# A macaron block (FFN, neighbourhood attention, FFN): new places for the value products, projections, sums and second FFN in the slot plan

## The chip, the cores and the metric

The kernel runs on one core of one Trainium2 chip. The metric is the device time of one execution in microseconds (us), lower is better. Before the change the median of three runs is 2293.7 us (2293.59 to 2294.9).

## The reference

The input is x, 4 batches of 4096 rows of 512 numbers. Three steps follow each other, each with a residual:

```python
x = x + 0.5 * ffn(layernorm(x))        # quantised to blocks of 32, one 512x512 matrix and a bias
x = x + attention(layernorm(x))        # 16 heads of 32; each row sees 13 neighbouring rows
x = x + 0.5 * ffn(layernorm(x))        # the same matrix and bias again
```

In `ffn` both operands are scaled in blocks of 32 to a 6-bit grid of values, multiplied back and then multiplied with each other. In `attention` q, k and v are 512x512 projections; the score of a row with each of its 13 neighbours gets a relative bias, softmax runs over the 13, the probabilities weight the neighbours' v, and a last 512x512 projection follows.

## The kernel before

**Tiling.** The 16384 rows are 128 tiles of 128 rows. Four tiles make a group of 512 rows; a group has four attention items, one for each set of four heads, so there are also 128 items. An item covers 16, 17 or 18 query blocks of 30 rows with windows of 42 keys.

**Exact products out of 16-bit halves.** Operands are split into a high and a low 16-bit part. `product` (line 137) makes one 128x512 result of 12 matmuls (three pairings of parts, four slices of 128). A tile or item needs six such results: `pmf1` (first FFN), `pmv` (values), two `pmqk` (queries and keys of an item), `pmo` (output projection) and `pmf2` (second FFN). Besides there are the scores `ps` (L458, 64 to 72 small matmuls) and the weighted values `pv` (L549, as many). With 18 blocks `pv` is too small and a second result `pw` is taken from the same three buffers as the six products (`ps_m`, three PSUM buffers); `ps` and `pv` have places of their own.

**The slot plan.** The order of all work is written out. Time is cut into slots, seven to a step (`STEP = 7`), and in each step one tile and one item advance by one stage. A stage is a Python generator. `begin(slot, stage, rank)` enters it; within a slot stages run by rank, and `yield n, rank` puts the rest of a stage n slots later. Each engine gets its instructions in the order in which the slots issue them and works through its queue in that order; semaphores make it wait for data and for buffers. Line 607 sets the slots of a tile or item: first FFN `F1`, values `V`, query and key projection `QK`, scores `SC`, weighted values `PV`, output projection `OUT`, and the second FFN `F2` slots behind `OUT`. `out_slot` and `second_slot` place the last tiles by themselves.

**Who does what.** TensorE (PE) does the products. ScalarE (ACT) takes the high parts out of PSUM (L379, L307, L576), normalises (L226, L284), does the exponential (L511) and the copies of the probabilities (L522, L523). GpSimd (POOL) does the adds of biases to x (L610), the two scalings of the quantiser (L239, L244), the small norm factors (L179 to L188) and three passes over the scores (L509, L518, L525). VectorE (DVE) does the rest: low parts (L383, L308, L582, L197), residual adds out of PSUM (L272, L595), statistics (L173, L174), the block maxima and their reciprocals (L232 to L237), the score sums (L500, L503), maxima (L507) and the sums of the probabilities (L514 to L516). SyncE (SP) issues loads, stores and transposing transfers.

**The order in the middle of the kernel**, for one step, as the built program has it:

- PE: ps, pmo, pmqk0, pv, pmqk1, pmf1, pmv, pmf2
- DVE: L507, L173, L174, L595, L173, L174, L197 hlq, L197 hln, L383 qf, L582, L514, L515, L516, L383 qk, L232, L233, L237, L272 (pmf1), L173, L174, L308, L272 (pmf2), L500, L503
- POOL: L179, L182, L185 (second norm), L610, L244, L525, L509, L179, L182, L187, L188 (quantised norms), L610 after_b, L610, L518, L239

A buffer of `ps_m` is free when DVE has taken the low part or the sum out of it. In items of 16 or 17 blocks `pmf1` goes into the buffer that `pmo` held, `pmv` into that of `pmqk0`, `pmf2` into that of `pmqk1`, `pmo` into that of `pmf1`.

Of the kernel before, what the change touches and what calls it, by code (L numbers as in the profile page):

```python
# [63 lines left out]
def macaron_kernel(  # L64
# [67 lines left out]
    def bc(t, n):  # L132

        return t.unsqueeze(2).to_broadcast([t.shape[0], t.shape[1], n])
# [4 lines left out]
    def product(pm, lhs, rhs):  # L139

        n = 0
        for a, b in ((0, 1), (1, 0), (0, 0)):
            for c in range(KC):
                nc.tensor.matmul(  # L144
                    pm, lhs(a, c), rhs(b, c), start=(n == 0), stop=(n == 3 * KC - 1)
                )
                n += 1
# [7 lines left out]
    def begin(slot, stage, rank=5):  # L155
        slots.setdefault(slot, []).append((rank, stage))
# [159 lines left out]
    def span(j):  # L316

        q0 = min(j * QN, length - QN)
        return q0, min(max(q0 - NS, 0), length - KN)

    def kind(j):
        return 1 if j == 0 else 2 if j == n_blocks - 1 else 0

    def late(j):

        return QR - QN if j == n_blocks - 1 else 0
# [11 lines left out]
    def straight(n):  # L338

        return -(-n // 2)  # L340
# [5 lines left out]
    n_items = n_batch * NG * KC  # L346
    qk, probs, stacks = {}, {}, {}

    def item_of(m):

        g, c = divmod(m, KC)
        return g // NG, g % NG, c
# [88 lines left out]
    def softmax(m):  # L441

        b, g, c = item_of(m)
        j0, j1 = group_blocks[g]
        n = j1 - j0
        tq, tk = qk.pop(m)
        ps = ps_s.tile([P, 2, 2, 2, 256], F32, tag="s", name=f"ps{m}")
        half = straight(n)
        for a in range(half):
            for part, sides in ((0, 2), (1, 1)):  # L450
                for i in range(a, n, half):
                    q0, k0 = (KN + at - g * GT for at in span(j0 + i))
                    q0 -= late(j0 + i)
                    u, w = divmod(a, PSB)
                    for r in (0, 2 * D):
                        rows = slice(r, r + 2 * D)
                        o = r if i < half else 2 * D - r
                        nc.tensor.matmul(  # L458
                            ps[o : o + 2 * D, i // half, u, :sides, w * KN : (w + 1) * KN],
                            tq[rows, part, 2 * q0 : 2 * (q0 + QR)],  # L460
                            tk[rows, :sides, k0 : k0 + KN],
                            start=part == 0, stop=part == 1,
                        )

        yield 1, 9
        sf = sfp.tile([P, MAXB, KN], F32, tag="sf", name=f"sf{m}")

        both = sf[:, : 2 * half, :].rearrange("p (v w) k -> p v w k", v=2)

        def parts(special):  # L470

            for w, e in ((0, PSB), (PSB, half)):
                lone = [(v, x) for v, x in special if w <= x < e]
                for v, x in lone:
                    yield slice(v, v + 1), slice(x, x + 1), 2 + v
                two = min(e, n - half)
                w0 = w + (1 if (0, w) in lone else 0)
                two -= 1 if (1, two - 1) in lone else 0
                if w0 < two:
                    yield slice(0, 2), slice(w0, two), 0  # L480
                for v, x, y in ((0, two, e), (1, w, w0)):
                    y = min(y, (half, n - half)[v])
                    if x < y and not (v == 0 and (v, x) in lone):
                        yield slice(v, v + 1), slice(x, y), v

        def sums(v, w, side):

            u, x = divmod(w.start, PSB)
            t = ps[:, v, u, side, x * KN : (x + w.stop - w.start) * KN]
            return t.rearrange("p v (w k) -> p v w k", k=KN)  # L490

        special = []
        if kind(j0) == 1:
            special.append((0, 0))
        if kind(j1 - 1) == 2:
            special.append((1, n - half - 1))
        for v, w, k in parts(special):
            o = both[:, v, w, :]
            bias = table[:, k : k + v.stop - v.start, c, :].unsqueeze(2).to_broadcast(o.shape)
            nc.vector.tensor_tensor(o, sums(v, w, 0), bias, ALU.add)  # L500
        for v, w, _ in parts([]):
            o = both[:, v, w, :]
            nc.vector.tensor_tensor(o, o, sums(v, w, 1), ALU.add)  # L503
        yield 1, 2
        s = sf[:, :n, :]
        top = sm.tile([P, MAXB], F32, tag="top", name=f"top{m}")
        nc.vector.tensor_reduce(top[:, :n], s, AX.X, ALU.max)  # L507
        yield 1, 4
        nc.gpsimd.tensor_tensor(s, s, bc(top[:, :n], KN), ALU.subtract)  # L509
        yield 1, 9  # L510
        nc.scalar.activation(s, s, AF.Exp, scale=alpha)  # L511
        yield 1, 4
        total = sm.tile([P, MAXB], F32, tag="total", name=f"total{m}")
        nc.vector.tensor_reduce(total[:, :n], s, AX.X, ALU.add)  # L514
        nc.vector.reciprocal(total[:, :n], total[:, :n])  # L515
        nc.vector.tensor_tensor(total[:, :n], total[:, :n], p_scale[:, :n], ALU.mult)  # L516
        yield 1, 4
        nc.gpsimd.tensor_tensor(s, s, bc(total[:, :n], KN), ALU.mult)  # L518
        yield 2, 8
        p = p_tile  # L520
        ph = p[:, :n, :KN]
        nc.scalar.copy(ph, s)  # L522
        nc.scalar.copy(p[:, :n, 2 * KN : KV], ph)  # L523
        yield 2, 4
        nc.gpsimd.tensor_tensor(p[:, :n, KN : 2 * KN], s, ph, ALU.subtract)  # L525
        pT = ptp.tile([P, MAXB, P], F16, tag="pT", name=f"pT{m}")
        nc.sync.dma_start_transpose(out=pT[:, :n, :], in_=p[:, :n, :].rearrange("p n k -> p (n k)"))
        probs[m] = pT
# [58 lines left out]
    def project_out(t, slot):  # L587

        r = t * P % RING
        pm = ps_m.tile([P, dim], F32, tag="mm", name=f"pmo_{t}")  # L590
        product(
            pm, lambda s, c: ring[:, s, c, r : r + P], lambda s, c: wt[:, s, c, PO : PO + dim]
        )
        yield 1, 8
        nc.vector.scalar_tensor_tensor(xs[t], pm, cp, xs[t], ALU.mult, ALU.add)  # L595
        moments(slot, t, "n3")

    def second_half(t):

        yield from ffn(t, "f2")  # L600
        nc.sync.dma_start(out=of[t * P : (t + 1) * P, :], in_=xs.pop(t))


    EARLY = 3
    STEP = 7

    F1, V, QK, SC, PV, OUT, F2 = 5, 2 * STEP + 6, 5 * STEP + 3, 6 * STEP, 8 * STEP + 3, 13 * STEP + 2, 12

    def add_bias(t, b):
        nc.gpsimd.tensor_tensor(xs[t], xs[t], b, ALU.add)  # L610
# [8 lines left out]
    HELD = range(NT - 15, NT - 7)  # L619
    LAST = NT - GROUP - 1  # L620

    def out_slot(t):


        i = t - LAST
        if i >= 0:
            return (n_items - 1) * STEP + PV + 3 + 2 * i
        if i >= 1 - GROUP:
            return LAST * STEP + PV + 21 + 4 * i
        return t * STEP + OUT  # L630

    def second_slot(t):

        i = t - LAST
        if t in HELD:
            return (n_items - 1) * STEP + PV - (16, 13, 10, 6, 5, 4, 3, 2)[t - HELD[0]]
        if i in (-2, -1):
            return out_slot(NT - 1) + 3 + i
        return out_slot(t) + F2

    for t in range(NT):
        k = t * STEP
        sooner = (0, 2, 5, STEP)[t] if t <= EARLY else 0
        begin(k - 18 - (STEP if t == EARLY else 0), one(load, t), 0)
        slot = k - 10 - (10 if t == EARLY else 0)
        enlist(slot, t, "n1")
        if not 0 < t < EARLY:
            begin(slot - 1, one(moments, slot, t, "n1"), 1)
        begin(k + F1 - sooner, first_half(t))
        begin(k + V, values(t))  # L650
        begin(k + F1 - sooner, one(add_bias, t, half_ffn_b), 8)
        at = out_slot(t)
        begin(at - 5, one(add_bias, t, after_b), 8)
        enlist(at + 2, t, "n3")
        begin(at, project_out(t, at + 2))
        begin(at + 6 if t < LAST else second_slot(t) - 2, one(add_bias, t, half_ffn_b), 8)
        begin(second_slot(t), second_half(t))
    for slot in together:
        if together[slot][0][0][1] == "n3" or together[slot][0][0][0] >= EARLY:
            begin(slot, quantised_norms(slot), 1)  # L660
    for m in range(n_items):
        k = m * STEP
        begin(k + QK, project_qk(m))
        begin(k + SC, softmax(m), 6)
        begin(k + PV, attend(m), 6)
    for n in range(n_batch * NG):
        k = n * GROUP * STEP
        b, g = divmod(n, NG)
# [4 lines left out]
    with tc.tile_pool(name="setup", bufs=1) as sp, tc.tile_pool(name="scratch", bufs=2) as scr:  # L673
# [23 lines left out]
        for o in chunks:  # L697
            w, i = (qkv_w, o) if o < 3 * KC else (proj_w, o - 3 * KC)
# [145 lines left out]
        for turned in (0, 2):  # L844
            for h in range(4):
                at = row_of(h ^ turned)
# [41 lines left out]
        slot = first  # L888
# [49 lines left out]
```

## Time and profile before

| what | us |
|---|---|
| median of three runs | 2293.7 |
| the profiled execution | 2295.28 |
| its span, which the profile shows | 2293.5 |
| PE busy in the span | 2214.2 (97%) |
| DVE busy | 2011.7 (88%) |
| POOL busy | 1969.2 (86%) |
| ACT busy | 1695.5 (74%) |
| chain of work that ended last: PE's share | 87% |

The mean granted clock of PE in the profiled execution is 0.993 of full speed. In the lists that follow a line gives the start in us from the beginning of the span, the busy time, the engine, the source line and the operation with output and inputs; `xN` counts merged instructions, and a bracket tells idle time just before and who ended it.

### The profile page before, as it was taken

The page shows a single profiled execution, that of the slowest core. Times are in us where ns is not written, and L with a number is a line of the kernel's source. Part 1 is how long each engine was busy: PE and PEld are TensorE (multiplying, and loading weights), DVE is VectorE, ACT ScalarE, POOL GpSimd, SP SyncE. Part 2 cuts the span into 40 slices and gives each one's busy share as a digit, 9 for nine tenths or more (in the row PEclk, how much of TensorE's full clock was granted, in tenths as well). Part 3 has the DMA queues.
Part 4 walks back from the last instruction along what each step waited for, and adds up shares of the span by engine and source line. Part 5 has one row for each costly group of instructions (what it writes and reads, how often), then busy time and mean ns, then how long its engine had stood idle before and what let it go on. Part 6 is the DMA issues. An engine that isn't in the chain of part 4 may idle for free.

```text
span 2293.5 us, 65425 instructions
## 1 busy us (share of the span) xinstructions
PE 2214.2 (97%) x26771; PEld 1052.9 (46%) x26771; DVE 2011.7 (88%) x3769; ACT 1695.5 (74%) x2544; POOL 1969.2 (86%) x2006
## 2 busy tenths in 40 slices
PE   3799999999999999999999999999999999999978
PEld 1344444444444444444444444444444444444433
DVE  6899998888988988898988998888988988989775
ACT  5697777777777777777777777777777777777752
POOL 4588988988988988888888888888888889888776
PEclk9999999999999999999999999999999999999989
DMA  7687776777767777777776776777776777866654
GB/s 201 153 178 161 162 160 154 159 162 158 160 156 155 164 162 154 161 158 157 162 158 155 162 161 154 160 157 155 164 160 151 167 158 154 166 155 147 137 107 104
DMA packets 926213, 359.61 MB, mean 157 GB/s; under 512 B 719452, under 2 KB 890328, under 8 KB 925912
## 3 DMA queue, kind: packets, MB, share of 16 engines
q1 hardware_dynamic: 925568, 354.90, 70.8%
q8 instruction: 209, 3.42, 0.6%
q14 instruction: 92, 0.75, 0.1%
q10 hardware_dynamic: 344, 0.53, 0.1%
HBM read 110.26 MB, written 67.29 MB: 77 GB/s over the span
## 4 chain that ended last, share of the span: by engine, by line
PE 87%; DVE 7%; ACT 2%; POOL 2%; DMA 1%; issue 1%; SPq 0%; ACTq 0%; DVEq 0%; POOLq 0%
PE pmqk L144 27%; PE pmf L144 26%; PE pmo L144 14%; PE pmv L144 13%; PE ps L458 4%; PE pv L549 3%; DVE stn L173 1%; DVE hlq L197 1%; DVE hln L197 1%; DVE sc L232 1%; ACT qk L390 0%; DVE x L272 0%; POOL yq L239 0%; DVE total L514 0%; DVE qf L383 0%
## 5 line engine op out<-in xcount | busy, mean ns | idle before, releaser
L144 PE MATMUL pmf<-wt,xT 128*128 128x512 f16 x3048 | 702.7, 381 | 13.3 <-DMA xT<-hlq 7.4
L144 PE MATMUL pmqk<-x,wt 128*128 128x512 f16 x3072 | 705.8, 379 | 0.4 <-DVE after_b L836 0.4
L144 PEld LDWEIGHTS <-xT 128*128 128x128 f16 x3048 | 298.4, 98 | 377.2 <-DMA xT<-hlq 15.2
L144 PEld LDWEIGHTS <-wt 128*128 128x128 f16 x3072 | 289.7, 98 | 336.0 <-issue 1.3
L239 POOL TENSOR_TENSOR yq<-yq,r 128x1024 f32<-128x1024 f32 (+1 forms) x141 | 247.1, 1752 | 135.6 <-DVE r L237 124.1
L144 PE MATMUL pmv<-wt,x 128*128 128x512 f16 x1536 | 353.9, 380 | 4.2 <-DVE qf L383 2.6
L144 PE MATMUL pmo<-wt,ring 128*128 128x512 f16 x1536 | 357.2, 383 | 0.0
L390 ACT ACTIVATE qk<-qf,parity 128x1024 f16<-128x1024 f16 x256 | 349.3, 1432 | 0.0
L610 POOL TENSOR_TENSOR x<-x,half_ffn_b 128x512 f32<-128x512 f32 x256 | 327.8, 1281 | 0.0
L272 DVE SCALAR_TENSOR_TENSOR x<-pmf,coef,x 128x512 f32<-128x512 f32 x256 | 180.0, 703 | 144.7 <-PE pmf L144 141.1
L576 ACT ACTIVATE ring<-pv 128x510 f16<-128x510 f32 (+7 forms) x176 | 78.7, 475 | 307.3 <-PE pv L549 234.4
L173 DVE BATCH_NORM_STATS2 stn<-x 128x6 f32<-128x512 f32 x384 | 265.2, 691 | 8.8 <-DMA x<-in_L_attn_x_dram 0.2
L244 POOL TENSOR_TENSOR yq<-q,sc 128x1024 f32<-128x1024 fp8e4 (+1 forms) x141 | 246.2, 1746 | 4.8 <-ACT q L242 4.8
L144 PEld LDWEIGHTS <-x 128*128 128x128 f16 x1536 | 150.5, 98 | 186.9 <-issue 4.9
L242 ACT ACTIVATE q<-yq,nudge 128x1024 fp8e4<-128x1024 f32 (+1 forms) x141 | 150.0, 1064 | 115.9 <-POOL yq L239 107.6
L144 PEld LDWEIGHTS <-ring 128*128 128x128 f16 x1536 | 141.2, 98 | 160.5 <-issue 5.0
L518 POOL TENSOR_TENSOR sf<-sf,total 128x714 f32<-128x714 f32 (+2 forms) x128 | 178.7, 1396 | 37.2 <-DVE total L516 19.3
L226 ACT ACTIVATE yq<-x,nbq,rsq 128x512 f32<-128x512 f32 x254 | 193.1, 803 | 16.7 <-POOL nbq L185 15.2
L525 POOL TENSOR_TENSOR p<-sf,p 128x714 f16<-128x714 f32 (+2 forms) x128 | 192.5, 1504 | 0.0
L509 POOL TENSOR_TENSOR sf<-sf,top 128x714 f32<-128x714 f32 (+2 forms) x128 | 182.4, 1425 | 3.5 <-DVE top L507 3.3
L197 DVE TENSOR_TENSOR hlq<-yq,hlq 128x1024 f16<-128x1024 f32 (+1 forms) x141 | 167.6, 1189 | 8.7 <-ACT hlq L193 6.6
L610 POOL TENSOR_TENSOR x<-x,after_b 128x512 f32<-128x512 f32 x128 | 162.9, 1274 | 0.0
(143 smaller groups left out, 3441.0 us busy)
## 6 DMA issues: line engine op xcount, KB each, us to landing
vs<-vd SPq DMA_DIRECT2D x144, 357.0 KB
x<-in_L_attn_x_dram SPq DMA_DIRECT2D x128, 256.0 KB
vd<-vt SPq DMA_DIRECT2D x128, 256.0 KB
out_dram<-x SPq DMA_DIRECT2D x128, 256.0 KB
vs<-vd SPq DMA_DIRECT2D x24, 378.0 KB
vs<-vd SPq DMA_DIRECT2D x24, 315.0 KB
rows<-in_L_attn_qkv_w_dram SPq DMA_DIRECT2D x12, 256.0 KB
xT<-hlq SPq DMA_TRANSPOSE x141
```

The source lines that it names most:

```text
L144: nc.tensor.matmul(pm, lhs(a, c), rhs(b, c), start=(n == 0), stop=(n == 3 * KC - 1))
L173: nc.vector.bn_stats(st, xs[t])
L197: nc.vector.tensor_tensor(hl[:, :, 1, :], y, hl[:, :, 0, :], ALU.subtract)
L226: nc.scalar.activation(y[:, u], xs[t], AF.Identity, bias=nb[:, u : u + 1], scale=rs[:, u : u + 1])
L239: nc.gpsimd.tensor_tensor(yb, yb, bc(r, QB), ALU.mult)
L244: nc.gpsimd.tensor_tensor(yb, q8.rearrange("p u (n q) -> p (u n) q", q=QB), bc(sc, QB), ALU.mult)
L272: nc.vector.scalar_tensor_tensor(xs[t], pm, cf, xs[t], ALU.mult, ALU.add)
L390: nc.scalar.activation(to, whole[0], AF.Copy, scale=parity[:, e : e + 1])
L509: nc.gpsimd.tensor_tensor(s, s, bc(top[:, :n], KN), ALU.subtract)
L518: nc.gpsimd.tensor_tensor(s, s, bc(total[:, :n], KN), ALU.mult)
L525: nc.gpsimd.tensor_tensor(p[:, :n, KN : 2 * KN], s, ph, ALU.subtract)
L610: nc.gpsimd.tensor_tensor(xs[t], xs[t], b, ALU.add)
```

## The change

Every stage keeps its instructions; their places in the plan change.

- `attend` (pv) starts at `9 * STEP` in place of `8 * STEP + 3`, with rank 7: right behind the scores of the item three later. For the last three items it starts four slots sooner than that.
- `project_out` starts two slots later (`OUT`), with rank 7, behind `second_half`, which comes four slots later (`OUT` and `F2` by two each), with rank 6. Both now stand behind the second `pmqk`.
- In `softmax` the sums of the probabilities come one slot later, the copies three (one of them from the sums, two more), the low part four.
- The quantised norm of a new tile comes two slots later (from tile 4 on).
- The last tiles keep their places: `LAST_PV` holds the old value of `PV`, `82` and `12` replace expressions that would have moved.

The orders in the middle of the kernel, as the built program has them:

- PE: ps, pv, pmqk0, pmqk1, pmf2, pmo, pmf1, pmv
- DVE: L507, L197 hln, L383 qf, L173, L174, L272 (pmf2), L595, L173, L174, L383 qk, L197 hlq, L514, L515, L516, L272 (pmf1), L173, L174, L308, L232, L233, L237, L500, L503, L582
- POOL: L179, L182, L185 (second norm), L239, L509, add of half_ffn_b, L244, add of half_ffn_b, L179, L182, L187, L188 (quantised norms), add of after_b, L525, L518

`pmo` now goes into the buffer that `pmqk0` of the same step held, `pmf1` into that of `pmf2`, `pmv` into that of `pmo`; in items with 18 blocks `pmf2` goes into the buffer of `pw`, elsewhere into that of `pmv`.

```diff
@@ softmax
         nc.scalar.activation(s, s, AF.Exp, scale=alpha)
-        yield 1, 4
+        yield 2, 4
         total = sm.tile([P, MAXB], F32, tag="total", name=f"total{m}")
...
         nc.gpsimd.tensor_tensor(s, s, bc(total[:, :n], KN), ALU.mult)
-        yield 2, 8
+        yield 4, 8
         p = p_tile
...
-        yield 2, 4
+        yield 3, 4
         nc.gpsimd.tensor_tensor(p[:, :n, KN : 2 * KN], s, ph, ALU.subtract)
@@ the plan
-    F1, V, QK, SC, PV, OUT, F2 = 5, 2 * STEP + 6, 5 * STEP + 3, 6 * STEP, 8 * STEP + 3, 13 * STEP + 2, 12
+    F1, V, QK, SC, PV, OUT, F2 = 5, 2 * STEP + 6, 5 * STEP + 3, 6 * STEP, 9 * STEP, 13 * STEP + 4, 14
+
+    LAST_PV = (n_items - 1) * STEP + 8 * STEP + 3
@@ out_slot
-            return (n_items - 1) * STEP + PV + 3 + 2 * i
+            return LAST_PV + 3 + 2 * i
-            return LAST * STEP + PV + 21 + 4 * i
+            return LAST * STEP + 82 + 4 * i
@@ second_slot
-            return (n_items - 1) * STEP + PV - (16, 13, 10, 6, 5, 4, 3, 2)[t - HELD[0]]
+            return LAST_PV - (16, 13, 10, 6, 5, 4, 3, 2)[t - HELD[0]]
-        return out_slot(t) + F2
+        return out_slot(t) + (F2 if t < LAST else 12)
@@ entering the stages
-        slot = k - 10 - (10 if t == EARLY else 0)
+        slot = k - (8 if t > EARLY else 20 if t == EARLY else 10)
-        begin(at, project_out(t, at + 2))
+        begin(at, project_out(t, at + 2), 7)
-        begin(second_slot(t), second_half(t))
+        begin(second_slot(t), second_half(t), 6)
-        begin(k + PV, attend(m), 6)
+        begin(k + (PV if m < n_items - 3 else PV - 4), attend(m), 7)
```

## The prediction

> **What bounds the kernel now.** I read the busy times first, then the stretches of 100 us, then one step of the middle in order of time. Busy share and stretches (sums of PE, weight loads, DVE, ACT, POOL; clock; DMA):
>
> ```profile
> PE 2214.2 (97%) x26771; PEld 1052.9 (46%) x26771; DVE 2011.7 (88%) x3769; ACT 1695.5 (74%) x2544; POOL 1969.2 (86%) x2006
> ```
>
> ```profile
> 1000.00:1100.00 100.00, 100.00 (x1242) 47.85 (x1240) 89.57 (x166) 76.58 (x114) 89.22 (x88) 1.00 0.72 157
> ...
> 2200.00:2300.00 100.00, 78.71 (x744) 35.44 (x744) 61.17 (x111) 34.08 (x52) 65.91 (x73) 0.92 0.42 96
> ```
>
> In the middle PE never rests, so a step lasts as long as PE's own work: pmo starts at 1001.53, the next at 1018.65, 17.11 us apart, at full clock. DVE and POOL have about a tenth left; only the end is loose. One step, in order of time:
>
> ```profile
> 1001.53 2.76 PE L144 MATMUL pmo<-wt,ring 128*128 128x512 f16 x12
> ...
> 1004.14 2.75 PE L144 MATMUL pmqk<-x,wt 128*128 128x512 f16 x12
> ...
> 1006.82 0.69 PE L549 MATMUL pv<-pT,vs 126*32 126x30 f16 x68
> 1006.86 1.20 DVE L197 TENSOR_TENSOR hlq<-yq,hlq 128x1024 f16<-128x1024 f32 x1
> 1007.03 1.08 POOL L179 TENSOR_SCALAR rsq<-mv 128x2 f32<-128x2 f32 x1 [0.16 <-DVE mv L174]
> ...
> 1007.45 2.76 PE L144 MATMUL pmqk<-x,wt 128*128 128x512 f16 x12
> ...
> 1007.98 0.68 DVE L197 TENSOR_TENSOR hln<-yn,hln 128x512 f16<-128x512 f32 x1
> ...
> 1008.20 1.04 POOL L182 TENSOR_TENSOR rsq<-rsq,minus_half 128x2 f32<-128x2 f32 x1
> ...
> 1008.92 0.75 DVE L383 SCALAR_TENSOR_TENSOR qf<-pmqk,qk_b,qf 128x512 f16<-128x512 f32 x1 [0.26 <-ACT qf L379]
> ...
> 1009.78 1.27 POOL L610 TENSOR_TENSOR x<-x,after_b 128x512 f32<-128x512 f32 x1
> ...
> 1010.04 2.75 PE L144 MATMUL pmf<-wt,xT 128*128 128x512 f16 x12
> ...
> 1010.19 0.89 DVE L514 TENSOR_REDUCE total<-sf 128x17 f32<-128x714 f32 x1
> ...
> 1011.01 1.27 POOL L610 TENSOR_TENSOR x<-x,half_ffn_b 128x512 f32<-128x512 f32 x1
> 1011.11 0.27 DVE L515 RECIPROCAL total<-total 128x17 f32<-128x17 f32 x1
> ...
> 1011.41 0.91 DVE L516 TENSOR_TENSOR total<-total,p_scale 128x17 f32<-128x17 f32 x1
> ```
>
> Two things matter. A product followed by a product takes 2.59 (1007.45 to 1010.04); followed by pv it takes 2.68 (1004.14 to 1006.82). And L516, 17 numbers a partition, is busy 0.91, up to 0.04 after POOL's add ends (1012.28). In the drained end, with POOL idle, and over all 128:
>
> ```profile
> 2183.07 0.18 DVE L516 TENSOR_TENSOR total<-total,p_scale 128x18 f32<-128x18 f32 x1
> ```
>
> ```profile
> L516 DVE TENSOR_TENSOR total<-total,p_scale x128: 175/894/1279, 105.6 to 2230.8; 128x17 f32<-128x17 f32 x80, 128x18 f32<-128x18 f32 x32, 128x16 f32<-128x16 f32 x16
> ```
>
> (minimum/median/maximum in ns). So L516 waits for the POOL instruction under way, up to 1.10 us. The reverse shows too: L179 takes 1.08 under L197, but 0.19 at 1016.86 without it.
>
> **The change, part by part.**
>
> *PE's own work.* Nothing is added; pv moves from between two products to behind ps. One change from product to small matmuls goes: 0.09 an item. The change back (pv's 0.63 and ps's 0.73 hold about 0.12 of it, the gap from the last ps at 1001.42 to pmo) is replaced by ps to pv, which no row shows. Bounds: all of the 0.12 stays, or it goes too (pv to pw, in one layout, starts after 0.008). The gain is thus 0.09 to 0.20; I take 0.10, since ps and pv use the array in different shapes (64\*64, 126\*32) as product and pv do. PE alone would make 17.01 a step.
>
> The Trainium skill, "TensorEngine Tiling (Array Packing)", section Key Properties, speaks against more: a change of tiling mode, not merely of tile, drains the array, and ps to pv is such a change. By that rule three of the four changes an item stay and the sum is the low end; without it, the high end.
>
> *The new queue of DVE, and a ring through PE.* This decides. After the change pmo goes into the buffer of its own step's pmqk0, so it waits for L383 qf. In DVE's new order, L595, which empties pmo, stands ahead of everything up to the next L383 qf. So pmo, L595, the rest of DVE's queue, L383 qf, pmo is a closed ring. Before, the reader of qf's buffer was pmv, at 1012.63, 2.96 after L383 qf ended (1009.67), and slack covered it. The ring's length from start-to-start times in this step: L595 0.76, L173 0.73, L174 0.10, L383 qk 0.66, L197 hlq 1.12, L514 0.92, L515 0.30, L516 0.10 without a wait (as at 2183.07), L272 0.68, L173 0.73, L174 0.10, L308 0.59 (0.67 less the 0.08 by which neighbours overlap), L232 1.24, L233 0.23, L237 0.27, L500 0.95, L503 0.94, L582 0.60, L507 0.82, L197 hln 0.60, L383 qf 0.75: 13.19. With pmo's 2.76 and two semaphores (0.05, 0.04) the ring is 16.04. It stays hidden below PE's 17.01 only while its waits for POOL sum to under 0.97.
>
> *Waits in the ring.* L516: 0 to 1.10 by the row above. In the new order POOL's L182, L187, L188 and the add of after_b follow the end of an L197 as they do here: from 1008.66 to the add at 1009.78 is 1.12. L516 follows L197 hlq by 0.92 + 0.30 less 0.08 = 1.14. The add starts 0.02 ahead, so L516 meets nearly all of it: I take 1.10. L233 reads two SBUF inputs as L516 does; here it runs at 0.19 (1014.14) beside an idle POOL, afterwards beside L179 and L182 of the second norm (0.19 and 0.57): 0 to 0.57, I take 0.28. L197 hln now stands right behind L507, whose end also releases POOL's L509: DVE is first, so POOL loses some 0.4, which its tenth covers. L197 hlq: 0 (as here), at most L182's 0.57. Ring: 16.04 + 1.10 + 0.28 = 17.42, 0.31 above 17.11.
>
> The Trainium skill, "SBUF — State Buffer", section "SBUF: two separate sides", says the port pair of DVE and POOL is an exclusive lock held for a whole instruction, whoever starts first. That would give L516 no wait at all if it came 0.02 sooner: ring 16.32 by that turn, hidden; 17.42 by the row.
>
> *Items with 18 blocks* (32 of 128). There pmf2 must wait for L582 of pw, before pmo: L507, L197, L383 (2.17) leave the ring, a product (2.59) enters, +0.42, for about 24 items in the middle.
>
> *SP and the softmax moves.* The sums, copies and low part move 1, 3 and 4 slots, pv four: the transposing transfer of p has the time to pv that it had, and loads of value stacks find their buffer free in the slot plan. DMA share 0.72: I cost it at nothing; if a stack were late, about 3 us each in 64 (the longest wait of pv for vs was 3.0).
>
> *Ramp and end.* Steps of the first eight items last 11 to 13 us and DVE queues there too: 0 to 1.3 more each (the two waits), I take 5 in all. In the end pmf2 and pmo now stand where PE waited 4.09 for ACT's L390 (two such gaps), but the last pv come together later: -8 to +12, I take +4.
>
> *Sum.* Middle items, 16 to 124: 108 x 0.31 = 33; 18 blocks 24 x 0.42 = 10; ramp 5, end 4: +52 on the span of 2293.5. The profiled execution (2295.28) lies 1.8 above its span and 1.6 above the median 2293.7, so the difference goes onto the median: 2346, rounded to 2344 as the near tie will not go the bad way every time.
>
> **The rivals.** *PE stays the bound* (the gain arrives). For it: PE is at 100% and a hidden ring costs nothing; the tie at L516 is 0.02 wide. Against: with PE as bound DVE drifts against POOL, and L516 or L197 meets another add. Time: 2293.7 - 117 x 0.10 (0.09 to 0.20: 10.5 to 23) + 9 for ramp and end = 2291, from 2279 to 2299 (with up to 16 there). It holds if ring waits stay under 0.97.
>
> *Half of it:* L516 waits its old median, 0.89 - 0.18 = 0.71, L233 0.28: ring 17.03, so only items with 18 blocks (24 x 0.4) and ramp and end pay, less 108 x 0.08: about 2304. For it: that is what L516 does now. Against: the order around it is new.
>
> *It does not do what it says:* no; the built order has pv behind ps in every item.
>
> *Worse:* POOL, 89% busy, with L509 and L182 held by L197, closes a ring too; L516 1.10, L233 0.57, L197 0.57 give 18.28, +126. For it: POOL's slack is only a tenth; against: all three at once in every step.
>
> **How the numbers follow.** No change that a measurement of this kernel can tell is within 0.2%, 2289.1 to 2298.3. Long ring 0.62 (own range 2316 to 2364; 2316 is L516 1.10 and L233 without a wait: ring 17.14, +3, and 19 for blocks, ramp and end), half 0.20, PE bound 0.13, worse 0.05. Of the PE-bound case 0.07 is faster, 0.05 same, the rest slower; half gives 0.02 same. Together faster 0.07, same 0.07, slower 0.86. The range runs from 2293, within the PE-bound case, to 2364, where L233 waits its whole 0.57 (108 x 0.29 = 31 above the sum, of which I keep 18).
>
> **What would show it.** Right: the middle's steps 17.3 to 17.6 apart, PE below 100% with its idle time before pmo released by DVE L383 qf, L516's median above 1.1, L233 above 0.19, pv 0.1 sooner behind ps than behind a product. Wrong: PE at 100% with steps near 17.0, or idle time before another line (a transfer, L390, POOL).

## The result, and the profile after

The changed kernel takes 2310.8 us (median of four runs, 2310.5 to 2315.1) against 2294.3 of the kernel before on the same chip (2293.6 to 2295.0): ratio 1.0079, interval 1.0066 to 1.0091. It is slower, by 16.5 us, where 50 were forecast. The profiled run took 2310.68 and its span is 2308.7, 15.2 above the span of before.

The busy times of the changed kernel, first part of the page:

```profile
PE 2208.2 (96%) x26771; PEld 1064.1 (46%) x26771; DVE 1950.2 (84%) x3769; ACT 1688.9 (73%) x2544; POOL 1932.6 (84%) x2006
```

PE has the same instructions and is busy 6.0 us less while the span is 15.2 longer, so its idle time grew by 21. Where the loss lies is told by the starts of `ps` in the two timelines (us between the starts of the items named):

| stretch | before | after | difference |
|---|---|---|---|
| start to item 0 | 97.2 | 97.9 | +0.7 |
| items 0 to 8 | 97.1 | 107.2 | +10.2 |
| items 8 to 16 | 138.8 | 141.1 | +2.3 |
| items 16 to 124 | 1839.3 | 1837.9 | -1.4 |
| item 124 to the end | 121.1 | 124.6 | +3.5 |

The middle, where the forecast had its loss, is even a little shorter; the ramp lost. The waits of PE over the whole span (total, times, longest, in us):

```profile
PE ps L458 <- ACT qk L390: 21.6, 13, 3.6
...
PE pv L549 <- DMA pT<-p: 5.9, 1, 5.9
PE pv L549 <- issue: 5.8, 4, 2.9
...
PE pmo L144 <- DVE qf L383: 0.6, 2, 0.5
```

The wait that was forecast, of `pmo` for L383 qf, is the last line: 0.6 us in all. Three others are the story: `ps` for L390 (12.7 before), the last `pv` but one for its transposed probabilities, and "issue", idle time that no semaphore explains.

One step of the middle in order of time (start, busy time, in us):

```profile
1004.08 0.75 DVE L383 SCALAR_TENSOR_TENSOR qf<-pmqk,qk_b,qf 128x512 f16<-128x512 f32 x1
...
1005.41 2.75 PE L144 MATMUL pmo<-wt,ring 128*128 128x512 f16 x12
...
1008.20 0.75 DVE L595 SCALAR_TENSOR_TENSOR x<-pmo,coef,x 128x512 f32<-128x512 f32 x1 [1.84 <-PE pmo L144]
...
1010.26 0.71 POOL L182 TENSOR_TENSOR rsq<-rsq,minus_half 128x2 f32<-128x2 f32 x1
...
1010.45 1.22 DVE L197 TENSOR_TENSOR hlq<-yq,hlq 128x1024 f16<-128x1024 f32 x1
...
1012.00 1.27 POOL L612 TENSOR_TENSOR x<-x,after_b 128x512 f32<-128x512 f32 x1
...
1012.81 0.50 DVE L516 TENSOR_TENSOR total<-total,p_scale 128x17 f32<-128x17 f32 x1
```

`pmo` starts 0.58 after L383 qf ends (1004.83): the ring has slack, and DVE idles 1.84 ahead of L595. The add of after_b starts 0.81 ahead of L516, not 0.02 as forecast, so L516 meets only its tail and takes 0.50.

The ramp, item 5 (order of time):

```profile
154.40 0.89 DVE L507 TENSOR_REDUCE top<-sf 128x17 f32<-128x714 f32 x1
...
155.36 1.76 POOL L509 TENSOR_TENSOR sf<-sf,top 128x714 f32<-128x714 f32 x1 [2.07 <-DVE top L507]
...
157.16 0.89 ACT L511 ACTIVATE sf<-sf,coef 128x714 f32<-128x714 f32 x1 [0.71 <-POOL sf L509]
...
157.96 0.67 ACT L379 ACTIVATE qk<-pmqk,qk_b 128x512 f16<-128x512 f32 x1
...
159.03 2.73 ACT L390 ACTIVATE qk<-qf,parity 128x1024 f16<-128x1024 f16 x2
...
161.81 0.78 PE L458 MATMUL ps<-qk 64*64 64x84 f16 x66 [1.63 <-ACT qk L390]
```

This is a second ring: from `ps` of one item (148.05) over L500 (152.01), L503, L507, POOL's L509 and ACT's queue (L511 stands ahead of L379, and that ahead of L390) to the next `ps`, whose first two matmuls ran at 159.96 and which goes on at 161.81, 0.05 after L390. It is 13.8 long. The same ring in the kernel before:

```profile
155.25 0.81 PE L458 MATMUL ps<-qk 64*64 64x84 f16 x68
...
157.28 1.02 DVE L500 TENSOR_TENSOR sf<-ps,table 128x504 f32<-128x504 f32 x3
...
164.31 2.72 ACT L390 ACTIVATE qk<-qf,parity 128x1024 f16<-128x1024 f16 x2
...
167.15 0.81 PE L458 MATMUL ps<-qk 64*64 64x84 f16 x68
```

It is 11.9 long; `ps` follows L390 by 0.12, without idle time of PE, whose own products cover the ring. After, L197 hlq and the sums (145.69 to 148.81) stand on DVE ahead of L272, L173, L308 and L232 to L237, and all of these still come between `ps` and L500, which starts 4.0 behind `ps` in place of 2.0; and L509 is held by L197 hln (1.39 became 1.76). In the middle, where a step is 17.01, L390 ends at 1012.20 and `ps` starts at 1013.27: 1.07 of slack.

The third loss, in the middle (item 23):

```profile
466.05 0.69 PE L549 MATMUL pv<-pT,vs 126*32 126x30 f16 x67
...
468.64 0.18 PE L549 MATMUL pv<-pT,vs 126*32 126x30 f16 x1 [1.90 <-issue]
```

PE stops 1.9 us within one `pv`, between two matmuls that wait for nothing. The page's list of DMA queues has a line for the loading of instructions:

```profile
q8 instruction: 209, 3.42, 0.6%
```

209 transfers of 3.42 MB are 16 KB each; PE's 26771 weight loads and 26771 matmuls over 209 are 256 instructions each. Counted in the built program, the matmul after this stop is PE's instruction 9405. The other stops of this kind stand at 19902, 31165, 33726, 39613, 43710, 47549 and so on: each of them is 189 or 190 modulo 256, thirteen between 190 and 2150 us, where PE passes 188 such places. So PE stands at the seam of two blocks. The block for this stop began to come at 465.78 and had landed at 467.21; PE went on 1.43 later (1.24 to 1.50 in the thirteen). With `ps` and `pv` back to back PE uses 272 instructions in 1.4 us; before, no block of 256 lasted under 4 us, and its trace has one stop of this kind, 0.5 us.

The Trainium skill, "Runtime: NRT & Kernel Launch", section "Instruction fetch mechanics", has the 16 KiB blocks of 256 instructions and says that crossing one is mostly hidden, since dispatch is slower than the refill. This trace agrees with the blocks; the hiding holds at most seams and fails at thirteen of the 188, and in the middle these stops sum to 6.9 us.

### The profile page after: what moved, and what is told of

Its sections match the earlier page's. It is cut to its first block, busy times and chain, and to the rows that moved or that the text cites. A ratio compares the mean times of both kernels' runs of the same rounds, so it can differ in the third digit from the quotient of the medians.

```text
span 2308.7 us, 65644 instructions
## 1 busy us (share of the span) xinstructions
PE 2208.2 (96%) x26771; PEld 1064.1 (46%) x26771; DVE 1950.2 (84%) x3769; ACT 1688.9 (73%) x2544; POOL 1932.6 (84%) x2006
## 3 DMA queue, kind: packets, MB, share of 16 engines
q8 instruction: 209, 3.42, 0.6%
## 4 chain that ended last, share of the span: by engine, by line
PE 85%; DVE 6%; POOL 3%; issue 2%; ACT 2%; DMA 2%; SPq 0%; POOLq 0%; DVEq 0%; ACTq 0%
PE pmqk L144 26%; PE pmf L144 26%; PE pmo L144 13%; PE pmv L144 12%; PE ps L458 4%; PE pv L549 3%; POOL sf L509 1%; ACT qk L390 1%; DVE stn L173 1%; POOL x L612 1%; DVE sf L500 1%; DVE hlq L197 1%; POOL yq L244 1%; DMA pT<-p 1%; DVE sc L232 0%
## 5 line engine op out<-in xcount | busy, mean ns | idle before, releaser
L144 PE MATMUL pmqk<-x,wt 128*128 128x512 f16 x3072 | 691.9, 382 | 2.9 <-issue 2.9
L144 PEld LDWEIGHTS <-xT 128*128 128x128 f16 x3048 | 298.3, 98 | 380.1 <-DMA xT<-hlq 17.8
L509 POOL TENSOR_TENSOR sf<-sf,top 128x714 f32<-128x714 f32 (+2 forms) x128 | 225.1, 1759 | 166.6 <-DVE top L507 166.6
L390 ACT ACTIVATE qk<-qf,parity 128x1024 f16<-128x1024 f16 x256 | 350.7, 1436 | 0.0
L612 POOL TENSOR_TENSOR x<-x,half_ffn_b 128x512 f32<-128x512 f32 x256 | 327.7, 1280 | 0.0
L595 DVE SCALAR_TENSOR_TENSOR x<-pmo,coef,x 128x512 f32<-128x512 f32 x128 | 95.9, 749 | 227.5 <-PE pmo L144 227.5
L173 DVE BATCH_NORM_STATS2 stn<-x 128x6 f32<-128x512 f32 x384 | 265.4, 691 | 9.9 <-DMA x<-in_L_attn_x_dram 1.3
L239 POOL TENSOR_TENSOR yq<-yq,r 128x1024 f32<-128x1024 f32 (+1 forms) x141 | 247.1, 1753 | 25.6 <-DVE r L237 19.8
L284 ACT ACTIVATE yn<-x,nbn,rsn 128x512 f32<-128x512 f32 x128 | 104.1, 814 | 203.3 <-POOL nbn L185 203.3
L244 POOL TENSOR_TENSOR yq<-q,sc 128x1024 f32<-128x1024 fp8e4 (+1 forms) x141 | 246.2, 1746 | 5.3 <-ACT q L242 5.3
L193 ACT CAST hlq<-yq 128x1024 f16<-128x1024 f32 (+1 forms) x141 | 135.3, 960 | 148.4 <-POOL yq L244 142.7
L144 PEld LDWEIGHTS <-ring 128*128 128x128 f16 x1536 | 150.0, 98 | 183.1 <-issue 2.6
L272 DVE SCALAR_TENSOR_TENSOR x<-pmf,coef,x 128x512 f32<-128x512 f32 x256 | 190.0, 742 | 30.9 <-PE pmf L144 27.1
L525 POOL TENSOR_TENSOR p<-sf,p 128x714 f16<-128x714 f32 (+2 forms) x128 | 193.1, 1509 | 0.0
L518 POOL TENSOR_TENSOR sf<-sf,total 128x714 f32<-128x714 f32 (+2 forms) x128 | 179.2, 1400 | 3.1 <-DVE total L516 3.1
```

Source lines behind the costliest of these rows:

```text
L144: nc.tensor.matmul(pm, lhs(a, c), rhs(b, c), start=(n == 0), stop=(n == 3 * KC - 1))
L173: nc.vector.bn_stats(st, xs[t])
L239: nc.gpsimd.tensor_tensor(yb, yb, bc(r, QB), ALU.mult)
L244: nc.gpsimd.tensor_tensor(yb, q8.rearrange("p u (n q) -> p (u n) q", q=QB), bc(sc, QB), ALU.mult)
L272: nc.vector.scalar_tensor_tensor(xs[t], pm, cf, xs[t], ALU.mult, ALU.add)
L390: nc.scalar.activation(to, whole[0], AF.Copy, scale=parity[:, e : e + 1])
```

## The experiments

All were timed beside the kernel before. Stretches are as in the table above.

**One part at a time.** `pv_only`: the kernel before with the move of pv alone.

```diff
-    ... PV, OUT, F2 = ... 8 * STEP + 3, 13 * STEP + 2, 12
+    ... PV, OUT, F2 = ... 9 * STEP, 13 * STEP + 2, 12
+    LAST_PV = (n_items - 1) * STEP + 8 * STEP + 3
...
-        begin(k + PV, attend(m), 6)
+        begin(k + (PV if m < n_items - 3 else PV - 4), attend(m), 7)
```

> The kernel before with the move of pv alone (pv behind ps, rank 7; four slots sooner for the last three items). Theory 'three places': the change gains 0.10 us a step in the middle from pv behind ps, loses some 6 us there to stalls of PE between blocks of 256 instructions (ps and pv together are 272 and last 1.4 us), and loses the rest in ramp and end through the other moves. Then this kernel has the gain and the stalls without the losses: middle steps 17.01, eight to twelve stalls of PE without a semaphore, first eight steps 97 to 99 as before, time 2287 to 2294, about 2290. Rival 'ring' (the prediction's): the loss comes from pmo behind L383 qf, which is not here: no stalls, 2283. Rival 'pv behind ps is the loss': 2305 to 2311.

2316.5 us, ratio 1.0096 (1.0082 to 1.0109). The ramp is as expected (98.9 for items 0 to 8), but the middle is 17.8 longer than before, so the theory missed there. In this order `pmo` stands right behind `pv`, and the `pmo` of every fourth tile stops within its product (some 7 us in all), mostly until DVE's L582 of that `pv`; stops at seams cost 15; and in two stretches of 3.4 us, after stops, the granted clock is 0.50 and 0.51 and the matmuls of `pmo` come 0.43 us apart in place of 0.22 (3 us in all).

`out_old`: the changed kernel with output projection, second FFN and norms at their old places (pv and softmax moved).

```diff
-    ... 9 * STEP, 13 * STEP + 4, 14
+    ... 9 * STEP, 13 * STEP + 2, 12
...
-        slot = k - (8 if t > EARLY else 20 if t == EARLY else 10)
+        slot = k - 10 - (10 if t == EARLY else 0)
-        begin(at, project_out(t, at + 2), 7)
+        begin(at, project_out(t, at + 2))
-        begin(second_slot(t), second_half(t), 6)
+        begin(second_slot(t), second_half(t))
```

> The changed kernel with output projection, second FFN and norms at their old slots and ranks: pv and softmax moved, nothing else. Theory 'three places': middle 17.01 with the stalls, ramp within 4 us of before, the late pT at the end stays: 2291 to 2299, about 2295. Rival 'ring': pmo's place is what costs, and without it 2283. Rival 'the softmax moves are the loss': 2305 or more.

2387.7 us, 1.0404 (1.0390 to 1.0418). All the theories missed. The waits of PE between 350 and 2150 us have it:

```profile
PE pmo L144 <- DVE ring L582: 41.4, 22, 3.0
```

The median step is 17.01, but 41 of 108 are over 17.25: the wait of `pv_only`, larger. Of the 27 products `pmo` with a stop of over 1 us inside, 26 are the last of a group of four tiles, and the stop is ahead of the eighth matmul, the first to read the low part of the group's fourth item in `ring`: that tile needs rows which the `pv` just ahead of it has filled, and L582 writes their low parts. So the later place of `pmo` (two slots of `OUT`, rank 7, the second FFN ahead of it), which I had read as a mere shift, is what gives L582 its time; the run undoes these together, with the norms, so it doesn't say how much of it each of them does. Without them the moves of pv and softmax cost 94 us over the kernel before. `out_old` and `pv_only` differ by the softmax slots alone: at the old place of `pmo` the later softmax costs 71 us more.

`soft_old`: the changed kernel with the old slots of the softmax.

```diff
-        yield 2, 4
+        yield 1, 4
-        yield 4, 8
+        yield 2, 8
-        yield 3, 4
+        yield 2, 4
```

> The changed kernel with the slots of the softmax as before (sums one slot, copies two, low part two). Theory 'three places': the wait of the last pv for pT (5.9) goes, and in the ramp L514 to L516 no longer stand ahead of L500, so the chain from ps over L500, L507, L509, L511, L379 and L390 to the next ps gets shorter: first eight steps 107.2 to about 102. Time 2297 to 2302. Rival 'the softmax moves cost nothing' (as predicted): 2311. Rival 'norms' (the later quantised norm of a new tile makes the ramp): end only, 2305.

2356.0 us, 1.0271 (1.0257 to 1.0285). Ramp and end came as expected (101.4 for items 0 to 8; 120.2 from item 124 on), the middle did not: steps of 17.58. PE's wait between 350 and 2150 us, and one of the steps:

```profile
PE pmf L144 <- DVE x L272: 42.1, 101, 0.7
```

```profile
1016.53 0.89 ACT L511 ACTIVATE sf<-sf,coef 128x714 f32<-128x714 f32 x1 [1.06 <-POOL sf L509]
...
1017.46 0.90 DVE L514 TENSOR_REDUCE total<-sf 128x17 f32<-128x714 f32 x1 [0.72 <-ACT sf L511]
...
1018.69 0.94 DVE L516 TENSOR_TENSOR total<-total,p_scale 128x17 f32<-128x17 f32 x1
...
1019.55 0.74 DVE L272 SCALAR_TENSOR_TENSOR x<-pmf,coef,x 128x512 f32<-128x512 f32 x1
...
1020.34 2.75 PE L144 MATMUL pmf<-wt,xT 128*128 128x512 f16 x12 [0.41 <-DVE x L272]
```

The sums (L514 to L516) stand ahead of L272, whose end frees the buffer of the next `pmf`; DVE waits for the exponential, L516 waits for POOL, PE waits for L272. With the other moves in place, the softmax moves, which the prediction costed at nothing, are what keeps this shut.

`n1_ramp`: the changed kernel with the norms of tiles 4 to 14 at the old slot.

```diff
-        slot = k - (8 if t > EARLY else 20 if t == EARLY else 10)
+        slot = k - (8 if t > 14 else 20 if t == EARLY else 10)
```

> The changed kernel with the quantised norm of tiles 4 to 14 at its old slot (there it has no partner anyway). Rival 'norms': the ramp's 13 us come back, 2298. Theory 'three places': only L197 and its POOL factors leave the stretch ahead of L500, some 0.7 of a step in eight steps, so 2304 to 2308; the first eight steps 102 to 105, the waits of ps for L390 not gone.

2303.8 us, 1.0044 (1.0032 to 1.0057): items 0 to 8 take 102.7, `ps` still waits 8.0 for L390 in the ramp. The norms are a part of the ramp's loss, not the whole.

**Is the forecast ring there, and how long is it?** `probe` puts one more reduction behind L516 in every item, `probe_half` over half the blocks, `kick` two of them in items 24 and 72 alone. The result goes to a place that is not read.

```diff
         nc.vector.tensor_tensor(total[:, :n], total[:, :n], p_scale[:, :n], ALU.mult)
+        nc.vector.tensor_reduce(top[:, :n], s, AX.X, ALU.add)                      # probe
+        nc.vector.tensor_reduce(top[:, : n // 2], s[:, : n // 2], AX.X, ALU.add)   # probe_half
+        for _ in range(2 if m in (24, 72) else 0):                                 # kick
+            nc.vector.tensor_reduce(top[:, :n], s, AX.X, ALU.add)
```

> The changed kernel with one more VectorE reduction of 0.92 us behind L516 in every item (the sums of the probabilities once more, into a place that is not read). Theory 'the ring is there and only L516's wait was too large': the ring is 16.04 plus 0.32 of L516's wait, 16.36, or 16.47 by the 0.54 us that pmo starts after L383 qf ends; with 0.92 it is 17.28 to 17.39, so steps of 17.3 to 17.4 in the middle, PE idle ahead of pmo released by L383 qf, and a time 29 to 45 above the changed kernel's 2311: 2340 to 2356. Rival 'no such ring' (VectorE is busy 84% and has the room): steps stay at 17.0 and the time within 5 of 2311.

2413.7 us, 1.0521 (1.0506 to 1.0535): 103 more than the changed kernel, over twice what was expected. `pmo` waits 48.6 us for L383 qf, in 60 items, and the median step there is 18.08. One step (the added line makes L613 of L612):

```profile
1010.20 2.75 PE L144 MATMUL pmo<-wt,ring 128*128 128x512 f16 x12 [0.91 <-DVE qf L383]
...
1015.24 1.22 DVE L197 TENSOR_TENSOR hlq<-yq,hlq 128x1024 f16<-128x1024 f32 x1
...
1015.37 1.66 POOL L182 TENSOR_TENSOR rsq<-rsq,minus_half 128x2 f32<-128x2 f32 x1
...
1017.58 1.27 POOL L613 TENSOR_TENSOR x<-x,after_b 128x512 f32<-128x512 f32 x1
1017.60 1.29 DVE L516 TENSOR_TENSOR total<-total,p_scale 128x17 f32<-128x17 f32 x1
```

Here is the step that was forecast: L182 held by L197, the add 0.02 ahead of L516, L516 at 1.29 (1.28 forecast). The ring is 16.04 + 0.92 + 1.11 = 18.07, as measured to 0.01. So the ring is real; but L516's wait is not a property of the order: in the changed kernel L516 takes under 0.6 us in 107 of the 108 middle items; here it takes over 1.2 in 63, among them 49 of the 60 in which PE waits, and under 0.6 in 44.

> The same reduction over half the blocks, 0.48 us. Theory of the ring of 16.36 to 16.47: 16.84 to 16.95, still under PE's 17.01, so the median step stays at 17.01 and the time rises by no more than 8 (single waits, ramp). If the ring is longer than the sum says (over 16.6), steps of 17.1 or more and 2320 upward.

2358.8 us, 1.0280 (1.0266 to 1.0294). Missed: 48 more, though 16.36 + 0.48 lies under 17.01. L516 takes two values, under 0.6 us in 66 of the 108 middle items and over 1.2 in 41. The two commonest steps are 17.01 (with those just below it 42) and 17.68 to 17.76 (31), close to 16.04 + 0.48 + 1.11 = 17.63; the others lie between and above.

> The changed kernel with two more reductions of 0.92 us on VectorE behind L516, in items 24 and 72 alone. Theory 'two states': L516's wait depends on how far VectorE lags POOL, and the ring closed at full wait (16.04 + 1.11 = 17.15) is longer than PE's 17.01, so after a kick the steps don't fall back at once: they stay at 17.1 to 17.3 for at least ten items with L516 at 1.2 to 1.3, and PE waits for L383 qf in each; 2311 plus 4 to 16. Rival 'one state': two long steps (up to 1.3 longer) and 17.01 from the next item on; 2311 to 2314.

2314.3 us, 1.0092 (1.0078 to 1.0106). Between the two theories. After the first kick (step 18.22) L516 stays at 1.28 to 1.30 for three items and the steps at 17.28 to 17.33; both fall back where the items with 18 blocks begin (item 28), after one more step of 17.56. After the second it stays for two items. So the closed state of the changed kernel exists, close to the forecast 17.42, but it does not last.

**The place of pv against ps.** `pv_first`: the changed kernel with pv just ahead of ps.

```diff
-        begin(k + (PV if m < n_items - 3 else PV - 4), attend(m), 7)
+        begin(k + (PV if m < n_items - 3 else PV - 4), attend(m), 5 if m < n_items - 3 else 7)
```

> The changed kernel with pv just ahead of ps in place of just behind it (not for the last three items). ps and pv stay together, so the gain of 0.10 a step stays (17.01). Theory 'blocks of instructions': the stalls 1.4 us after a block has landed depend on how early the sequencer reaches the end of a block; pv's inputs are there early, while the first ps waits for ACT, so with pv ahead PE's sequencer gets into the run of small matmuls sooner and the stalls shrink from 7 in the middle to 0 to 4: 2303 to 2309. Rival 'the stalls come from the change of array layout from ps to pv': they stay at 7 or move with the order, always at the first pv or ps and not at a fixed place in a block of 256 instructions: 2311.

2299.6 us, 1.0027 (1.0016 to 1.0039): better than either theory said. All that is left of the stops between 350 and 2150 us is one line:

```profile
PE pmqk L144 <- issue: 0.2, 1, 0.2
```

The middle takes 1831.6, which is 7.7 less than before, and items 8 to 16 take 135.9 (before 138.8, changed kernel 141.1); items 0 to 8 stay at 107.3. Array layouts change as often as in the changed kernel, so these changes are not what stopped PE. The blocks are still as short (down to 1.17 us), but where their start could be matched with a transfer, the next block nearly always began to come before PE had entered the short one; in the stops over 1 us of the changed kernel it began 0.13 us or more after. That PE's sequencer runs on because `pv` waits for nothing, while the first `ps` waits for ACT, is argued from this and not shown.

**Putting the lost places back.** `combo`: the edit of `n1_ramp`, and the old softmax slots for items 0 to 7 and the last three.

> The changed kernel with old slots where the change lost: quantised norms of tiles 4 to 14 at their old slot, softmax at its old slots for items 0 to 7 and the last three. Theory 'ramp and end': the first eight steps as in the kernel with pv alone (98.9, where the changed kernel has 107.2), items 8 to 16 140 to 142, middle 1834 to 1838, from the last four scores to the end 120 to 121 (124.6): 2292 to 2298, equal to before within 0.2%. Rival 'each move only shifts the loss': 2300 to 2304, as the kernel with the norms alone.

2301.6 us, 1.0030 (1.0020 to 1.0040). Items 0 to 8 take 97.0, before 97.05: the ramp's loss in them is the softmax moves and the norms together (the run moves sums, copies and low part at once and doesn't tell them apart). Items 8 to 16 are no better (142.9). The end is no better either (125.8): the wait for pT is gone, but at the item where old and new places meet `ps` waits 8.8 for L390.

`best_a` adds the edit of `pv_first` to the old places in the ramp, and has copies and low part two slots later instead of four and three for the last three items; `best_b` leaves that last edit out; `best_c` has the whole softmax at its old slots for the last six:

```diff
-        yield 2, 4
+        yield (2 if 8 <= m < NT - 6 else 1), 4
-        yield 4, 8
+        yield (4 if 8 <= m < NT - 6 else 2), 8
-        yield 3, 4
+        yield (3 if 8 <= m < NT - 6 else 2), 4
```

> The changed kernel with pv just ahead of ps, the old slots in the ramp (norms of tiles 4 to 14, softmax of items 0 to 7), and for the last three items copies and low part two slots behind the one before in place of four and three. First eight steps 97, items 8 to 16 136 to 141, middle 1832, end 119 to 122 (the wait of 5.9 for the last pT gone): 2282 to 2290, about 2286, faster than both. If the end only shifts its wait to ps, 125 there and 2290; if ramp and pv's place don't add up, 2294 to 2299.

2292.0 us, 0.9991 (0.9983 to 1.0000): short of the 2286 that was expected. Ramp (97.6, 136.2) and middle (1832.7) came as hoped, the end stayed at 125.2: PE waits 12.9 there for L390, and at the `pv` that had waited 5.9 for pT it still sits idle for 3.5, for nothing that the profile names. (It starts 4.6 after the issue of a transfer of its value stack; in the kernel before the `pv` of that item started 4.5 after such an issue, and there the profile names the stack. That the stack is the cause here too is argued.)

> The same without the edit for the last three items: 3 to 5 more than with it if the late pT is what the end pays for, the same time if the end is bound elsewhere; about 2290.

2291.2 us, 0.9990 (0.9981 to 0.9999), with the wait for pT (5.9) back and the same time, though in the two profiled runs the end differs by 1.8 (127.0 here). So the earlier copies shorten that idle time from 5.9 to 3.5 and don't change the time; what the end would take without it, these two runs don't show.

> The best kernel so far (pv ahead of ps, old slots in the ramp, copies and low part early at the end) with the softmax at its old slots for the last six items in place of the early copies for the last three. In the kernel with the old softmax throughout, the stretch from ps of item 124 to the end was 120.2 against 125.2 in the best one. If that comes from the sums standing early at the end, 2286 to 2289; if the step where old and new places meet costs as much (as at the last three items of the kernel with old slots, where ps waited 8.8), 2290 to 2295.

2288.5 us, 0.9978 (0.9968 to 0.9988), end 120.5. It is the fastest of all, 5 us under before: items 0 to 8 96.2, 8 to 16 137.4, middle 1835.5. With `soft_old` (120.2) it shows that the new softmax slots are what the end pays for; which of the three, and by which wait, it doesn't show.

## Why the prediction was right or wrong

*The sign* was right, slower, and for a wrong reason. The likeliest case, "long ring" (2316 to 2364), did not occur; in the middle it was the rival "PE stays the bound" that came true, by the prediction's own sign (steps near 17.0, idle time ahead of L390). Its 2291 was passed by 9.5 us of stops and waits in the middle, which no case had, and by ramp and end, which lost 16.7 in place of 9. Of the 52 that were added up, the ring's 43 came to nothing; that the kernel is slower all the same is luck in the main.

*PE's own work*: right. 0.10 forecast; the median step went from 17.11 to 17.01, and the 95 steps of the 108 that got shorter gained 0.115 on average (10.9 us). The row that was missing is there now: from the last `ps` to the first `pv` it takes 0.115 (median in the middle), as from the last `ps` to `pmo` before (0.118), so all of the 0.12 stays. The low end of the range held, so the Trainium skill's rule ("TensorEngine Tiling (Array Packing)", Key Properties: a change of mode drains the array) fits the trace.

*The ring and its length*: right. 16.04 without waits is what `probe` gives back.

*L516, 1.10*: this is the step that failed. I took the phase between DVE and POOL from a queue that never rests ("from 1008.66 to the add at 1009.78 is 1.12"), that is, from a ring already closed, and concluded that it closes. With PE as the bound DVE idles 1.84 at L595 and POOL catches up: L182 starts at 1010.26, before L197 (1010.45) and not behind it, the add comes 0.33 after L197's end in place of 1.12, and L516 waits 0.50 - 0.18 = 0.32. Ring 16.36 by the sum; by the trace 17.01 less the 0.54 by which `pmo` starts late (0.58 less a semaphore's 0.04), 16.47: hidden. The 33 us of the middle were 0.6. The near tie was worked out rightly for the closed ring (`probe` has it at 0.02), but both states had to be tried, and the kernel starts in the other one. The Trainium skill's lock ("SBUF — State Buffer", "SBUF: two separate sides": whoever starts first holds the ports) agrees with `probe`, where POOL is first by 0.02 and DVE waits it out.

*L233, 0.28*: 0; its median is 0.191, as before.

*L197 hln*: POOL's L509 lost 0.37 (median 1.391 to 1.765), as forecast (0.4). "Which its tenth covers" holds in the middle; in the ramp it lies in the chain to the next `ps`.

*Items with 18 blocks, +10*: 0, for the same reason as L516: a ring 0.42 longer is 16.8 and still hidden.

*Ramp, +5*: +12.5 from item 0 to 16. I counted DVE's waits and missed a second ring. PE waits there 9.5 for L390 and L383 of `ps` and 4.4 at seams, where before it waited 1.9 in all, and its granted clock is lower (0.97 on average in the first 109 us from item 0 on, before 1.00; from 135.8 to 139.2 it is 0.50). `combo` shows the cause for items 0 to 8: with softmax and norms at their old slots the 10.2 are gone. (The edit of the norms alone brings 4.5 of them, that of the softmax alone 5.8.) In items 8 to 16 it is the seams: `pv_first` leaves 0.9 of their 4.4, and the stretch takes 135.9.

*End, +4*: +3.5, within the range. The softmax slots are the cause: at the old ones the end takes 120.2 (`soft_old`) and 120.5 (`best_c`). The 5.9 of the late pT is in it, but `best_a`, which shortens it to 3.5, is no faster than `best_b`. (Not all of the last tiles kept their places: with `82` the output projection of three of them stands two slots later than the old expression had it, 80. No run changes this alone.)

*SP and softmax at nothing*: wrong in both directions. The later softmax costs the ramp, and in the middle it saves 54 us (1837.9 against 1892.0 in `soft_old`) as long as `pmo` stands at its new place; at the old one it costs (`out_old`).

*Not in the sum at all*: the seams between blocks of instructions, 6.9 in the middle. With the two waits for L383 qf and other small ones they make the other 13 steps 9.5 longer, and give back that much of the 10.9.

## What to carry to other kernels

A wait whose size depends on the phase of two engines must be worked out once with the ring open and once with it closed; if the open one fits under the bound, start there, and ask how small a push closes it (here 0.48 us of work cost 48). An edit that looks like a companion shift may be what makes the main move possible: undoing the parts one by one cost 45 and 77 us more, where undoing a part only in the ramp, or in ramp and end, was a gain of 7 to 9. Ramp and end have shorter steps, so every ring that is hidden in the middle has to be checked against their length too.

## What was not expected of the hardware

- PE can starve for instructions. With 272 of them in 1.4 us it stopped at 13 of 188 seams of two blocks, until 1.24 to 1.50 us after the next block had landed, for up to 2.9 us; with the other of the two runs of small matmuls first, the stops in the middle shrank from 6.9 us to 0.3.
- The wait of a short VectorE instruction for POOL has two values in one kernel, 0.32 and 1.11 us in items of 17 blocks, and the same order of instructions can run in either.
- After some of its idle times PE's matmuls come 0.43 us apart in place of 0.22 for some time, so a stop can cost more than its length: in the step from 134.76 seven in a row, where the granted clock is 0.50 for 3.4 us.
